# More filler products and an earlier count at the start of layer 1 of a four-layer graph kernel

## The chip, the core and the metric

The kernel runs on one core of a Trainium2 chip. TensorE (PE in the profile) does matrix products, VectorE (DVE) and ScalarE (ACT) do arithmetic on 128 partitions, GpSimd (POOL) does the same more slowly, SyncE (SP) issues DMA transfers. Each engine takes its own instructions in order and waits on semaphores that other engines raise. The metric is the device time of one execution in microseconds, and less is better. The median of three runs before the change is 498.71 us, and they lie between 497.31 and 499.81.

## The reference, cut to what matters

There are four layers. Each adds a graph operation to `x` (3327 rows of 64) and normalises the rows; all use the same dense matrix `adj` (3327 x 3327).

```python
x = _layernorm(x + _L0_gnn_ref(L0_gnn_t, x, adj))        # only row statistics of x survive
x = _layernorm(x + _L1_gnn_ref(x, adj, att_W, att_b))    # hyperbolic attention
x = _layernorm(x + _L2_gnn_ref(x, adj, W))               # two rounds of adj @ x, tanh
x = _layernorm(x + _L3_gnn_ref(x, adj, weight, bias))    # weighted by rank of neighbours
...
def _L1_gnn_ref(x, adj, att_W, att_b):
    x_tan = _logmap0(x, C)
    left = x_tan @ att_W[:D] + att_b
    right = x_tan @ att_W[D:]
    adj_att = jax.nn.sigmoid(left + right.T) * adj
    x_local = _logmap(x[:, None, :], x[None, :, :], C)
    support_t = jnp.einsum('ij,ijd->id', adj_att, x_local)
    return _proj(_expmap(x, support_t, C), C)
```

Layer 1 needs, for every row, two products with the attention weights (`left` and `right`) and functions of the row's variance. Then it makes a weight for each pair of rows: a sigmoid times `adj` times a function of the angle between the two rows.

## The kernel before, in words

The 3327 rows are padded to 26 blocks of 128. Blocks `b` and `b + 13` stand side by side as two halves, so that 13 pairs of blocks fill 128 partitions when they are turned (transposed).

The first 15 us are a preparation, written in a fixed order for all engines (`manual_schedule`): the order in the program is the order on each engine. The steps that matter here, by line:

- L1218 to L1219: three products of the identity with `center_4`, 512 columns each, into a bank `idle` that nobody reads. They run while the rows `x0` are still being loaded.
- L1225 to L1228: VectorE sums the rows and makes `xc`, the centred rows, a half at a time.
- L1244: TensorE turns the pairs of blocks of `x0` into four banks `pt`, as groups of 4, 4, 4 and 1. ScalarE copies them into `xT` (L1253). Between the first copy and the other three ScalarE squares `xc` (L1252).
- L1256 to L1264: VectorE sums the squares to the variance `v`, makes three linear functions of it (`vq`), then `low` (rows with a small variance) and `lows`, their number on each partition.
- L1267 to L1278: for each of the 13 pairs TensorE multiplies a 128 x 128 piece of `xT` with `attw_c`, which has 4 columns. These are the narrow products, into `pr`. Ahead of the fourth group stands `n_low`, a product that adds `lows` over the partitions. After the first group and after the fourth stands one more product into `idle`, of 512 and 256 columns.
- L1280 to L1290: ScalarE takes a square root, VectorE makes `t` and `r2` from it, copies `n_low` to the integer `flag` (L1285), and makes `lf` and `rb`, which read `pr`.
- L1292 to L1299: VectorE makes some more columns of 26 numbers, ending in `gas` and `aa`.

L2110 loads `flag` into a register of every engine, and L2111 branches on it: with no small norm `near_sphere` runs. There VectorE scales `lj` by `gas` (L1553), TensorE turns `lf` (L1459, `prep_left` and `first_left`), `lj` (L1481), `ri` (L1505) and makes `first_wrong` (L1491) with ordinary products, and ScalarE copies each result out of PSUM (L1515), with a sigmoid (L1373) between the copies. After that comes the loop over 104 tiles: products (L1400), angle on ScalarE (L1409), gather on VectorE (L1420 to L1424), sigmoid on ScalarE and its product with `adj` on GpSimd (L1378), and accumulation on TensorE (L1444). Layers 2 and 3 follow.

Each float product is two instructions on TensorE, each with a weight load of its own (PEld); a transpose is one.

Of the kernel before, what the change touches and what calls it, by code (L numbers as in the profile page):

```python
# [10 lines left out]
F32 = mybir.dt.float32  # L11
# [4 lines left out]
ALU = mybir.AluOpType  # L16
AX = mybir.AxisListType
PSUM = bass.MemoryType.PSUM

P = 128  # L20
# [39 lines left out]
NEAR_VAR = 0.05  # L60
# [22 lines left out]
def kernel(  # L83
# [11 lines left out]
    nc = tc.nc  # L95

    const = ctx.enter_context(tc.tile_pool(name="const", bufs=1))
    small = ctx.enter_context(tc.tile_pool(name="small", bufs=2))
# [11 lines left out]
    ident = const.tile([P, P], F32, name="ident")  # L110
# [57 lines left out]
    real = const.tile([P, NB], F32, name="real")  # L168
# [29 lines left out]
    center_4 = center.unsqueeze(1).to_broadcast([P, 4, P])  # L198
# [30 lines left out]
    def stat(tag):  # L229
        return small.tile([P, NB], F32, tag=tag, name=tag)  # L230
# [43 lines left out]
    def by_half(v):  # L274

        return v.rearrange("p (n h) d -> p n h d", h=2)
# [913 lines left out]
    with tc.tile_pool(name="l1", bufs=1) as l1:  # L1190
# [14 lines left out]
        flag = l1.tile([1, 1], I32, name="flag")  # L1205
        xc = xpool.tile([P, NB, D], F32, tag="x", name="xc")
        vec, sca = nc.vector.tensor_tensor, nc.vector.tensor_scalar
        stt = nc.vector.scalar_tensor_tensor
        with tc.tile_pool(name="l1a", bufs=1) as l1a, tc.tile_pool(
            name="l1ap", bufs=1, space=PSUM  # L1210
        ) as l1ap:
            v = l1a.tile([P, NB], F32, name="v")
            sums = l1a.tile([P, NB], F32, name="sums")
            sq = l1a.tile([P, NB, D], F32, name="sq_c")
            xT = l1a.tile([P, HALF], F32, name="xT_0")

            idle = l1ap.tile([P, 4 * P], F32, name="idle")
            for _ in range(3):  # L1218
                nc.tensor.matmul(idle, ident, center_4, start=True, stop=True)  # L1219

            pw = l1ap.tile([P, 4], F32, name="pw")
            attw_c = l1a.tile([P, 4], F32, name="attw_c")
            halves = (slice(0, None, 2), slice(1, None, 2))
            for h in halves:
                nc.vector.tensor_reduce(sums[:, h], x0[:, h, :], axis=AX.X, op=ALU.add)  # L1225
            for h in halves:
                stt(
                    xc[:, h, :], sums[:, h].unsqueeze(2).to_broadcast([P, NBH, D]), -1.0 / D,  # L1228
                    x0[:, h, :], op0=ALU.mult, op1=ALU.add,
                )  # L1230
            for h, c in zip(halves, (x0, xc)):

                nc.gpsimd.tensor_tensor(
                    lj[:, h, : D - 1], c[:, h, : D - 1],
                    c[:, h, D - 1 : D].to_broadcast([P, NBH, D - 1]), ALU.subtract,
                )

            pr = l1ap.tile([P, NBH, 2, 2], F32, name="pr")
            turned = []
            for i, g in enumerate(range(0, NBH, 4)):  # L1240
                n = min(4, NBH - g)
                pt = l1ap.tile([P, 4 * P], F32, tag="pt", bufs=4, name=f"pt_x_{g}")
                for k in range(n):
                    nc.tensor.transpose(  # L1244
                        pt[:, k * P : (k + 1) * P],
                        by_half(x0)[:, g + k].rearrange("p h d -> p (h d)"), ident,
                    )
                if i == 1:
                    nc.tensor.matmul(pw, center, attw_dg, start=True, stop=True)
                    nc.scalar.copy(attw_c, pw)  # L1250
                    for h in halves:
                        nc.scalar.activation(sq[:, h, :], xc[:, h, :], AF.Square)  # L1252
                nc.scalar.copy(xT[:, g * P : (g + n) * P], pt[:, : n * P])  # L1253
                turned.append((g, n))
            for h in halves:
                nc.vector.tensor_reduce(v[:, h], sq[:, h, :], axis=AX.X, op=ALU.add)  # L1256
            sca(vq[:, 1], v, 0.81 / D, LN_EPS, ALU.mult, ALU.add)
            sca(vq[:, 0], v, MIN_VAR, None, ALU.max)
            sca(vq[:, 2], v, 0.81 / D - 0.81, LN_EPS, ALU.mult, ALU.add)

            low = stat("low")
            stt(low, v, NEAR_VAR, real, op0=ALU.is_lt, op1=ALU.mult)
            lows = small.tile([P, 1], F32, tag="lows", name="lows")
            nc.vector.tensor_reduce(lows, low, axis=AX.X, op=ALU.add)  # L1264
            root = l1a.tile([P, 2, NB], F32, name="root")
            n_low = l1ap.tile([1, 1], F32, name="n_low")
            for i, (g, n) in enumerate(turned):  # L1267
                if i == 3:
                    nc.tensor.matmul(n_low, lows, ones, start=True, stop=True)
                for k in range(g, g + n):  # L1270
                    nc.tensor.matmul(
                        pr[:, k].rearrange("p h t -> p (h t)"), xT[:, k * P : (k + 1) * P],
                        attw_c, start=True, stop=True,
                    )
                if i in (0, 3):
                    w = 2 if i else 4
                    nc.tensor.matmul(
                        idle[:, : w * P], ident, center_4[:, :w], start=True, stop=True  # L1278
                    )
            nc.scalar.activation(root, vq[:, :2], AF.Sqrt)  # L1280
            nc.scalar.activation(warm, ones, AF.Sigmoid)
            nc.vector.reciprocal(root, root)
            t = l1a.tile([P, 2, NB], F32, name="t")
            vec(t, vq[:, :2], root, ALU.mult)
            nc.vector.tensor_copy(flag, n_low)  # L1285
            vec(t, t, root, ALU.mult)
            stt(r2, t, -3.0, root, op0=ALU.add, op1=ALU.mult)
            prs = pr.rearrange("p n h t -> p (n h) t")
            stt(lf, prs[:, :, 0], -0.5 * LOG_NORM, r2[:, 0], op0=ALU.mult, op1=ALU.mult)
            stt(rb, prs[:, :, 1], -0.5 * LOG_NORM, r2[:, 0], op0=ALU.mult, op1=ALU.mult)  # L1290

            nc.vector.reciprocal(rq, vq[:, 1:])  # L1292
            sca(rb, rb, attb_sb, None, ALU.add)
            sca(s, r2[:, 1], -0.45, None, ALU.mult)
            vec(g1, vq[:, 2], rq[:, 0], ALU.mult)
            vec(ga, vq[:, 1], rq[:, 1], ALU.mult)
            vec(gas, ga, s, ALU.mult)
            sca(lj[:, :, D - 1], ga, 2.0, -1.0, ALU.mult, ALU.add)
            sca(aa, g1, -1.0, 1.0, ALU.mult, ALU.add)  # L1299
# [867 lines left out]
```

## Time and profile before

| what | value |
|---|---|
| median of three runs | 498.71 us |
| the profiled execution, its own time | 499.74 us |
| its span, first to last instruction | 498.0 us |
| TensorE busy | 480.5 us (96%) |
| VectorE, ScalarE, GpSimd busy | 349.2, 266.3, 196.8 us |
| mean granted TensorE clock | 0.981 |

Times within the span are given in us from its first instruction. The profiled execution took 1.74 us more than its span. A busy TensorE is one that has an instruction under way; a product of 4 columns and one of 512 both count as busy. The column PEclk is the share of the full TensorE clock that was granted. In the chain of waits each line is a stretch of work that released the next one; in groups and timelines "x8" is the number of instructions, and "<-" names what ended a wait.

### The profile page before, as it was taken

How to read it: one execution, taken by the hardware profiler on the slowest of the kernel's cores; microseconds unless marked ns; L12 is line 12 of the kernel's file. 1: busy time of each engine (PE TensorE's matmuls, PEld its weight loads, DVE VectorE, ACT ScalarE, POOL GpSimd, SP SyncE). 2: the span in 40 equal slices, each digit the busy share in tenths (PEclk: the TensorE clock that was granted, in tenths of full speed). 3: DMA queues.
4: the chain of work that ended last, by engine and by line, in shares of the span. 5: the costliest groups of instructions: out<-in, count | busy, mean ns of one | idle time of the engine just before them, and what ended most of it. 6: DMA issues, size and time to landing. Idle time of an engine off the chain costs nothing.

```text
span 498.0 us, 7739 instructions
## 1 busy us (share of the span) xinstructions
PE 480.5 (96%) x2865; PEld 220.6 (44%) x2865; DVE 349.2 (70%) x600; ACT 266.3 (53%) x376; POOL 196.8 (40%) x175
## 2 busy tenths in 40 slices
PE   8999999999999999999999999999999999999991
PEld 4733333333333338643434353333345555555551
DVE  6698888878888887995363322656238999689743
ACT  4799999999999985400000000000016876666641
POOL 4299899989999991000000000000352274000000
PEclk9799999999999998999999999999999999999996
DMA  8988988887888278899999009988987699949001
GB/s 273 379 247 281 328 274 273 272 273 259 280 274 276 77 277 314 372 397 428 424 426 384 0 17 403 427 349 334 421 333 235 222 334 387 365 150 356 17 1 42
DMA packets 34186, 139.20 MB, mean 280 GB/s; under 512 B 11231, under 2 KB 13025, under 8 KB 29019
## 3 DMA queue, kind: packets, MB, share of 16 engines
q1 hardware_dynamic: 30603, 137.41, 73.9%
q0 software_dynamic: 1248, 0.64, 0.6%
q10 hardware_dynamic: 2288, 0.57, 0.6%
q8 instruction: 24, 0.39, 0.3%
q14 instruction: 23, 0.19, 0.1%
HBM read 136.93 MB, written 1.04 MB: 277 GB/s over the span
## 4 chain that ended last, share of the span: by engine, by line
PE 80%; DVE 8%; DMA 5%; issue 1%; ACT 1%; SPq 0%; POOL 0%; DVEq 0%
PE cnt L517 26%; PE pq L1400 17%; PE acc L1444 16%; PE cnt L651 5%; PE acc L883 5%; DMA at_l<-in_adjT 3%; PE acc L900 2%; DMA ah<-in_adjT 2%; PE t L452 2%; DVE mask L368 2%; DVE w L667 1%; PE both L752 1%; PE cnt L508 1%; PE pn_l L403 1%; PE pe L1735 1%
## 5 line engine op out<-in xcount | busy, mean ns | idle before, releaser
L1378 POOL TENSOR_TENSOR sg<-sg,at 128x832 f32<-128x832 f32 x88 | 131.2, 1519 | 7.6 <-ACT sg L1373 3.1
L517 PE MATMUL cnt<-at_l,lj 128*64 128x416 f32 x496 | 90.7, 515 | 0.8 <-DMA at_l<-in_adjT 0.8
L1373 ACT ACTIVATE sg<-lb,rb 128x1664 f32<-128x1664 f32 (+1 forms) x53 | 88.0, 1661 | 0.0
L1400 PE MATMUL pq<-riT,ljT 64*128 64x416 f32 x416 | 87.2, 536 | 0.2
L1444 PE MATMUL acc<-v,lj 128*64 128x416 f32 x416 | 85.1, 525 | 0.0
L1409 ACT ACTIVATE pq<-pq 128x832 f32<-128x832 f32 x104 | 83.8, 850 | 1.7 <-issue 1.6
L630 ACT ACTIVATE x<-cnt 128x416 f32<-128x416 f32 x8 | 4.1, 517 | 144.9 <-PE cnt L517 144.9
L669 ACT ACTIVATE w<-cnt 128x416 int16<-128x416 f32 x135 | 63.9, 520 | 28.3 <-PE cnt L651 26.8
L1424 DVE SCALAR_TENSOR_TENSOR v<-pq,sg 128x832 f32<-128x832 f32 x52 | 53.3, 1025 | 18.7 <-ACT pq L1409 18.3
L464 POOL DMA_DIRECT2D t_rows<-tb x4 | 4.1, 1045 | 151.0 <-DVE tb L462 151.0
L1400 PEld LDWEIGHTS pq<-riT,ljT 64*128 64x128 f32 x416 | 35.6, 186 | 49.5 <-ACT pq L1409 30.6
L517 PEld LDWEIGHTS cnt<-at_l,lj 128*64 128x64 f32 x496 | 34.3, 137 | 50.9 <-issue 48.6
L883 PE MATMUL acc<-w,s 128*128 128x416 bf16 x208 | 53.1, 339 | 0.0
L667 DVE TENSOR_SCALAR w<-cnt 128x416 int16<-128x416 f32 x73 | 42.1, 587 | 10.7 <-PE cnt L651 8.3
L1444 PEld LDWEIGHTS acc<-v,lj 128*64 128x64 f32 x416 | 26.0, 136 | 52.2 <-issue 48.4
L517 PE MATMUL cnt<-kept,lj 128*64 128x416 f32 x224 | 41.6, 514 | 0.0
L651 PE MATMUL cnt<-mask,tri 128*128 128x416 bf16 x136 | 35.6, 339 | 2.1 <-DVE w L667 2.1
L368 DVE TENSOR_SCALAR mask<-ah 128x1664 bf16<-128x1664 f32 x34 | 36.4, 1096 | 1.0 <-DMA ah<-in_adjT 1.0
L1421 DVE SCALAR_TENSOR_TENSOR pq<-pq,sg 128x416 f32<-128x416 f32 x52 | 31.2, 600 | 1.8
L445 DVE TENSOR_SCALAR tm<-at_l 128x1664 bf16<-128x1664 f32 x16 | 15.7, 1023 | 22.8 <-PE t L452 20.9
L1420 DVE SCALAR_TENSOR_TENSOR v<-pq,sg 128x416 f32<-128x416 f32 x52 | 30.2, 580 | 0.0
L1044 POOL DMA_DIRECT2D out<-hid x2 | 1.0, 514 | 73.3 <-DVE hid L1049 73.3
(321 smaller groups left out, 525.6 us busy)
## 6 DMA issues: line engine op xcount, KB each, us to landing
at_l<-in_adjT SPq DMA_DIRECT2D x27, 1664.0 KB, 12.3
at<-in_adjT SPq DMA_DIRECT2D x44, 832.0 KB, 5.8
ah<-in_adjT SPq DMA_DIRECT2D x34, 832.0 KB, 6.6
kept<-in_adjT SPq DMA_DIRECT2D x7, 1664.0 KB, 9.6
bt_l<-in_adjT SPq DMA_DIRECT2D x6, 1664.0 KB
lb<-lf_rows SPq DMA_DIRECT2D x2, 384.0 KB
mask<-t_rows SPq DMA_DIRECT2D x34, 3.2 KB
ljT<-ljT SPq DMA_DIRECT2D x4, 128.0 KB
```

What stands on the lines that cost most here:

```text
L368: nc.vector.tensor_scalar(mask[q], ahead.pop(q), 0.0, None, ALU.not_equal)
L517: nc.tensor.matmul(acc[c][h * D : (h + 1) * D, :], hw[:, slot(jb), :], blocks[jb][:, o : o + CW], start=c not in begun, stop=last, skip_gr ...
L651: nc.tensor.matmul(cnt[c][e], tri, mask[q][:, of], start=True, stop=True, skip_group_check=True,)
L667: nc.vector.tensor_scalar(to, of, 0.0, None, ALU.max)
L669: nc.scalar.activation(to, of, AF.Relu)
L883: nc.tensor.matmul(acc[h, c][:, e, :], s12[:, slot(jb)].rearrange("p t d -> p (t d)"), ws[q, c, e], start=first, stop=last,)
L1373: nc.scalar.activation(sg[:, :, of], lbs[:, :, of], AF.Sigmoid, bias=rb[:, sl : sl + 1])
L1378: nc.gpsimd.tensor_tensor(sg[:, h, of], sg[:, h, of], at[:, h, of], ALU.mult)
L1400: nc.tensor.matmul(pq[:, h, :], ljT[h != jb // NBH][rows, of], riT[rows, ch * CW : (ch + 1) * CW], start=True, stop=True,)
L1409: nc.scalar.activation(pqs[t], pqs[t], AF.Arctan, bias=ANGLE_FIRST, scale=ANGLE_STEP)
L1424: stt(w, pq, ANGLE_REST, sg, op0=ALU.add, op1=ALU.mult)
L1444: nc.tensor.matmul(accs[cp, ci][h * D : (h + 1) * D, :], lj[:, slot(jb), :], w[:, h, :], start=(jb == orders[cp][0]), stop=(jb == orders[c ...
```

## The change

The warm-up products at L1218 become 512, 512 and 256 columns instead of three times 512. `low` and `lows` are computed ahead of `vq[:, 1]`, `vq[:, 0]` and `vq[:, 2]` or between them. `n_low` stands ahead of the third group of narrow products instead of the fourth. In the second and third group a filler of 256 columns follows every second narrow product, four in all; the filler after the first group (512) and after the fourth (256) stay. VectorE copies `flag` before it makes `t` instead of after.

```diff
-            for _ in range(3):
-                nc.tensor.matmul(idle, ident, center_4, start=True, stop=True)
+            def filled(w=4):
+                nc.tensor.matmul(idle[:, : w * P], ident, center_4[:, :w], start=True, stop=True)
+
+            for w in (4, 4, 2):
+                filled(w)
...
+            low = stat("low")
+            lows = small.tile([P, 1], F32, tag="lows", name="lows")
+            stt(low, v, NEAR_VAR, real, op0=ALU.is_lt, op1=ALU.mult)
             sca(vq[:, 1], v, 0.81 / D, LN_EPS, ALU.mult, ALU.add)
             sca(vq[:, 0], v, MIN_VAR, None, ALU.max)
+            nc.vector.tensor_reduce(lows, low, axis=AX.X, op=ALU.add)
             sca(vq[:, 2], v, 0.81 / D - 0.81, LN_EPS, ALU.mult, ALU.add)
-
-            low = stat("low")
-            stt(low, v, NEAR_VAR, real, op0=ALU.is_lt, op1=ALU.mult)
-            lows = small.tile([P, 1], F32, tag="lows", name="lows")
-            nc.vector.tensor_reduce(lows, low, axis=AX.X, op=ALU.add)
             root = l1a.tile([P, 2, NB], F32, name="root")
             n_low = l1ap.tile([1, 1], F32, name="n_low")
             for i, (g, n) in enumerate(turned):
-                if i == 3:
+                if i == 2:
                     nc.tensor.matmul(n_low, lows, ones, start=True, stop=True)
                 for k in range(g, g + n):
                     nc.tensor.matmul(
                         pr[:, k].rearrange("p h t -> p (h t)"), xT[:, k * P : (k + 1) * P],
                         attw_c, start=True, stop=True,
                     )
-                if i in (0, 3):
-                    w = 2 if i else 4
-                    nc.tensor.matmul(
-                        idle[:, : w * P], ident, center_4[:, :w], start=True, stop=True
-                    )
+                    if i and k % 2:
+                        filled(2)
+                if i == 0:
+                    filled()
+                if i == 3:
+                    filled(2)
             nc.scalar.activation(root, vq[:, :2], AF.Sqrt)
             nc.scalar.activation(warm, ones, AF.Sigmoid)
             nc.vector.reciprocal(root, root)
+            nc.vector.tensor_copy(flag, n_low)
             t = l1a.tile([P, 2, NB], F32, name="t")
             vec(t, vq[:, :2], root, ALU.mult)
-            nc.vector.tensor_copy(flag, n_low)
             vec(t, t, root, ALU.mult)
```

## The prediction

> **What bounds the kernel now.** I first read the granted clock in short stretches of the opening, since the change adds products that nobody reads. Columns: busy us (and instructions) of PE, PEld, DVE, ACT, POOL, then PEclk, DMA share, GB/s.
>
> ```profile
> 4.55:7.96 3.41, 3.41 (x7) 1.35 (x6) 2.05 (x3) 0.00 (x0) 1.55 (x1) 1.00 1.11 259
> 7.96:11.37 3.41, 3.41 (x26) 2.62 (x24) 3.24 (x4) 3.02 (x6) 1.55 (x1) 1.00 1.00 418
> 11.37:14.78 3.41, 3.19 (x26) 2.77 (x26) 3.06 (x18) 2.14 (x5) 0.00 (x0) 1.00 0.98 401
> 14.78:18.20 3.42, 2.75 (x14) 2.35 (x13) 2.91 (x10) 2.16 (x3) 0.00 (x0) 0.50 1.07 334
> 18.20:21.61 3.41, 3.41 (x25) 2.75 (x23) 1.55 (x3) 1.93 (x4) 1.68 (x2) 0.50 0.97 406
> ...
> 192.28:195.69 3.41, 3.41 (x34) 3.41 (x33) 2.38 (x9) 1.86 (x5) 0.00 (x0) 1.00 0.76 218
> 195.69:199.10 3.41, 3.41 (x19) 3.41 (x18) 3.01 (x26) 2.06 (x8) 0.00 (x0) 0.50 0.97 408
> ```
>
> The clock is halved from 14.78 to 21.61 (6.83 us) and from 195.69 to 199.10 (3.41 us): both edges lie on one grid of 3.41 us, which I use for the stretches. The stretch ahead of each drop is nearly all "busy", but with narrow products. Then the chain of waits over the opening:
>
> ```profile
> 15.76 0.70 DVE lj L1553
> 16.46 0.04 issue
> 16.50 1.11 PE first_right L1481 x4
> 17.61 1.28 PE first_left L1459 x6
> 18.89 0.85 PE first_turn L1505 x4
> 19.75 1.91 PE first_wrong L1491 x16
> 21.65 0.59 PE first_turn L1505 x4
> ...
> 22.57 0.44 PE prep_fours L1481 x4
> ```
>
> TensorE at half clock is on the path: four transposes cost 0.85 to 1.11 us, and 0.44 at full clock. ScalarE then takes the copy of `first_wrong` at 21.70 and its sigmoids at 22.18, and from there the loop runs without a gap. Last, the narrow products and who reads them, in the timeline:
>
> ```profile
> 10.12 1.10 PE L1277 MATMUL idle<-both_m,ident 128*128 128x512 f32 x2
> 11.18 1.95 PE L1271 MATMUL pr<-attw_c,xT 128*128 128x4 f32 x16
> 13.06 0.19 PE L1269 MATMUL n_low<-ones,lows 128*1 128x1 f32 x2
> 13.18 0.39 PE L1271 MATMUL pr<-attw_c,xT 128*128 128x4 f32 x2
> ...
> 13.59 0.21 DVE L1287 SCALAR_TENSOR_TENSOR r<-t,root 128x52 f32<-128x52 f32 x1
> 13.91 0.19 DVE L1289 SCALAR_TENSOR_TENSOR lf<-pr,r 128x26 f32<-128x26 f32 x1
> ```
>
> The last narrow product ends at 13.57 and `lf` starts at 13.91: TensorE is only 0.34 us early. The end moves with this place: the loop's TensorE rows follow each other from 26.16 on, and at layer 1's end the chain goes from VectorE's last scaling into the transfer `at_l` (211.79, 13.94 us). So a shift at 22.18 reaches the end one for one.
>
> **The change, part by part.** *Shorter warm-up.* The first six filler instructions start about 0.85 us apart (5.49 us in all), so half of a product less ends them 0.85 sooner. The transposes of x can then start when x is there, at 6.85 (the weight load that waited for the DMA) instead of 7.47. That is worth nothing: ScalarE's squares wait for `xc`, ready at 8.75 and 9.73, and the other copies of `xT` follow them (10.56); so the second narrow group still starts at 11.18. Without that cover it would be a gain of 0.6.
>
> *The four fillers.* Full-clock price of 416 columns: the chain shows 32 such instructions of L517 in 5.74 us, two at a time, 0.36 a pair; 256 columns are 0.22, a filler of two 0.44. Its first weight load (16 loads of L1271 took 1.86, so 0.116 each) is exposed, and the one after it hidden, so no more is added. The upper bound is 0.68, the whole row of the old 256-column filler at L1277, its drain included; I take the stream, since here other work follows. Four: **1.77 us** of TensorE ahead of the last narrow product. VectorE's 0.34 of slack covers a part; `lf` needs 15.3 instead of 13.91: **+1.4 us**. Behind it on VectorE stand `rb`, the columns to `aa`, the branch and `lj` L1553; behind those TensorE's turns and ScalarE's copies and sigmoids. All move by 1.4.
>
> *Order of the count.* Short VectorE operations start 0.09 apart, so one put ahead of `vq` delays the root by 0.08; `lows` is ready 0.1 to 0.2 sooner. But `n_low` now stands behind the second group and two fillers: 11.18 + 8 x 0.116 + 0.88 = 12.99, and before it ran at 13.06. So `flag` comes at about 13.3 as before, and with it the register loads and the two `kept` transfers (SP issues them at 14.19): 0. VectorE waits there with `t` behind it, which was at 12.97: about 0.3 later, r2 at 14.0 to 14.1. The wait for `pr` until 15.3 hides all of it; without the fillers it would cost 0.2 to 0.3.
>
> *The clock.* What the fillers can buy: with full clock from 17.9 on (16.50 + 1.4), `first_right` 0.44, `first_left` 0.66, one turn 0.44 and `first_wrong` 0.96 end at 20.4; ScalarE's five copies and the wait for the first results (18.9, then copies 0.42 to 0.58 apart) end at 21.4. The sigmoid at 22.18 comes 0.8 sooner: saving 2.2, less the 1.4. If the clock falls just as now: +1.4. If it falls already among the fillers, each costs 0.88 and a narrow product twice its load: some 2 more, about +3.5.
>
> **Does the clock hold?** For each stretch I add the columns streamed (a 128-column transpose 0.11 at full clock, a product of 4 columns nothing). Share of 3.41 us with columns moving: 4.55 to 7.96 1.00 at half speed, and the clock rose; 7.96 to 11.37 0.60 (nine transposes and the 512 filler), it held; 11.37 to 14.78 0.27 (256 filler and four transposes), it fell; 14.78 to 18.20 0.70 at half speed, it stayed down; 18.20 to 21.61 0.90 at half speed, it rose; 192.28 to 195.69 0.17, it fell. So it drops somewhere between 0.27 and 0.60, and rises (half speed counted half) between 0.37 and 0.45. With one threshold for both it is about 0.4. After the change, on the same grid, 11.37 to 14.78 holds three fillers and part of the fourth, 1.57 us or 0.46, and the next 0.52 (the last filler, eight transposes, the first of `lj`). Just above: there the clock would hold.
>
> But the Trainium skill (TensorE: Matmul & The Clock Gate, Part 1) says that this window is free-running and does not start with the kernel. No row here shows a second grid; the three times before differ by 2.5 us, as they would. If the grid stands still, the sum is 499.74 - 0.8 = 498.9. If it moves, other windows count. The earlier transposes bring the 512 filler forward, to about 9.4 to 10.3 where the clock is already up. A window whose end lies from 11.9 to 12.6 then holds that filler and less than one small one, 0.25 to 0.38; one that ends from 13.3 to 14.5 holds two or three small ones and at most the rest of the large one, 0.26 to 0.39. Together that is 1.9 of 3.41 us: with the threshold at 0.4 the clock falls in nearly six of ten positions. And the execution shown was a bad one for the kernel before, 1.03 above the median: with edges at 13.1, 16.5 and 19.9 the clock is back for half of `first_wrong`, and 22.18 becomes 21.4. So against the median the clock that holds saves 0 to 0.2, and one that falls costs +1.4 to +3.5. I take the moving grid: four in ten at -0.1, six in ten spread over 1.4 to 3.5, and after the median over runs **+1.7: 500.4 us**.
>
> A second rule of that page (Part 4) speaks against the change more strongly: transposes do not count as work for the clock. Then the stretch after the fillers would be left with one filler (0.13 to 0.2) and the clock would fall at 18.2: +1.4. Here the row disagrees: without transposes 18.20 to 21.61 would be 0.50 and the clock rose, while the warm-up from 1.13 to 4.54 was 0.64 and it did not. I count them.
>
> **The rivals.**
> - *The clock holds in nearly every execution* (threshold near 0.3): 498.71 - 0.2 = 498.5, down to 497.5 if the position of the profiled run is common. For it: 0.46 and 0.52 against 0.27. Against it: the low windows at other positions. This one ends on the other side, and it decides once the lowest window's share lies above the threshold.
> - *The clock falls among the fillers, or never rises in the warm-up*: fillers at half clock give about +3.5, so 502.2. The warm-up's window loses 0.25 to 0.6 us of streaming, at half speed 0.42 to 0.46 instead of 0.50; if the rise needs more than that, everything to about 25 us runs at half clock, some +7, 505.7. For it: 0.45 is the least that raised the clock. Against it: 0.45 did.
> - *The fillers are free*, if `lf` were not waiting for TensorE: 498.71 - 2.2 = 496.5. Against it: 0.34 us of slack.
>
> **How the numbers follow.** A measurement of this kernel can tell about 0.5% (2.5 us) from no change. Forecast as told (some executions with the clock down, +0.5 to +3.2): 0.56, of which 0.14 over 2.5. Clock holds: 0.23, within 0.5%. Clock down among the fillers or in the warm-up: 0.18, nearly all over 2.5. Free fillers: 0.03, faster by about 0.5%. So faster 0.03, same 0.65, slower 0.32. The forecast's own range is 499.2 to 501.9; for 8 in 10 it reaches down into the held clock, 498.0, and up into the second rival, 503.0.
>
> **What would show it.** Four 256-column fillers in L1271's stretch, the last narrow product at about 15.1, `lf` at 15.3, and L1553 at about 17.2: the fillers' price. `n_low` near 13.1 and `flag` near 13.3: the reordering brings nothing. PEclk 1.00 from 8 to 25 with the sigmoid at 21.4 means that the clock holds; 0.50 anywhere from 12 to 22 means that it does not, and edges off 14.78 that the grid moves. I am wrong if `lf` stays before 14.3, if weight loads or fillers overlap more than I think, or if the loop absorbs the shift.

## The result, and the profile after

Over 22 executions of each kernel, taken side by side, the median went from 499.02 us to 500.09 us; the ratio is 1.0036 with a 95% interval of 1.0018 to 1.0053. (The ratios of this document are not quotients of medians: here that would be 1.0021, and the quotient of the means, 500.62 to 498.85, is 1.0035.) The change makes the kernel slower by a little, and the interval does not contain 1. The medians hide a change of shape: before, the executions lie evenly between 497.25 and 499.84. After, ten of 22 lie between 498.79 and 499.36, three between 500.09 and 500.63, and nine between 501.38 and 504.19. Those nine have a mean granted clock of 0.977 to 0.982 each, the other thirteen 0.987 to 0.993.

The profiled execution of the changed kernel took 499.36 us (span 497.6) and is one of the thirteen. The line numbers are 3 higher from here on. First the stretches of its clock grid, with the same columns as before (busy us of PE, PEld, DVE, ACT, POOL, then PEclk, DMA share, GB/s):

```profile
6.41:9.82 3.41, 3.14 (x25) 2.74 (x25) 3.41 (x4) 1.62 (x3) 1.20 (x1) 1.00 0.93 371
9.82:13.24 3.42, 2.67 (x15) 1.58 (x14) 2.96 (x9) 2.95 (x6) 1.55 (x1) 1.00 1.03 436
13.24:16.65 3.41, 3.31 (x24) 2.79 (x24) 1.78 (x12) 0.81 (x2) 0.00 (x0) 1.00 0.99 298
16.65:20.06 3.41, 2.49 (x23) 2.08 (x23) 2.94 (x9) 2.99 (x6) 0.00 (x0) 1.00 0.94 394
20.06:23.48 3.42, 3.38 (x33) 2.27 (x30) 3.09 (x6) 3.42 (x5) 1.93 (x2) 1.00 1.02 433
```

The clock stays full where it was halved before. The edges are not where they were: the clock rose at 6.41 in this execution, at 7.96 in the one before. (Ahead of that first rise PEclk reads 1.00 too, since the profile records the clock from its first change on; that TensorE runs at half clock there is seen from the warm-up, whose instructions of 512 columns start 0.85 us apart, against 0.47 in the run e4 below at full clock.) Then the path, from the timelines of TensorE, VectorE and ScalarE:

```profile
11.28 0.61 PE L1273 MATMUL pr<-attw_c,xT 128*128 128x4 f32 x4 [0.76 <-ACT xT L1256]
11.74 0.68 PE L1219 MATMUL idle<-both_m,ident 128*128 128x256 f32 x2
...
13.23 0.19 PE L1271 MATMUL n_low<-ones,lows 128*1 128x1 f32 x2
...
15.21 0.28 PE L1273 MATMUL pr<-attw_c,xT 128*128 128x4 f32 x2
```

```profile
13.46 0.15 DVE L1286 CAST flag<-n_low 1x1 int32<-1x1 f32 x1 [0.40 <-PE n_low L1271]
13.54 0.19 DVE L1288 TENSOR_TENSOR t<-vq,root 128x52 f32<-128x52 f32 x1
...
15.53 0.18 DVE L1292 SCALAR_TENSOR_TENSOR lf<-pr,r 128x26 f32<-128x26 f32 x1 [1.31 <-PE pr L1273]
...
17.38 0.68 DVE L1556 TENSOR_TENSOR lj<-lj,gas 128x504 f32<-128x504 f32 x1 [0.47 <-DVE aa L1302]
```

```profile
20.93 0.58 ACT L1518 COPY ljT<-first_wrong 128x512 f32<-128x512 f32 x1
21.42 2.57 ACT L1376 ACTIVATE sg<-lb,rb 128x832 f32<-128x832 f32 x2
```

`lf` now waits 1.31 us for TensorE, and starts at 15.53 instead of 13.91. What the fillers cost is in that bracket. The full clock then gives time back: from `lf` to the start of ScalarE's second sigmoid, the 21.42 above, it takes 5.89 us instead of 8.27, and this sigmoid starts 0.76 sooner than before (22.18). Not all of that reaches the end. The last product into `acc`, at the end of layer 1's loop, ends 0.32 sooner (190.63 against 190.95), and the span is 0.4 shorter. The missing 0.45 appears at VectorE's first `v` of the loop, here before and after the change:

```profile
25.60 1.02 DVE L1424 SCALAR_TENSOR_TENSOR v<-pq,sg 128x832 f32<-128x832 f32 x1 [0.20 <-ACT pq L1409]
25.29 1.02 DVE L1427 SCALAR_TENSOR_TENSOR v<-pq,sg 128x832 f32<-128x832 f32 x1 [0.65 <-ACT pq L1412]
```

It starts 3.42 us after the second sigmoid before, and 3.87 after. The experiments show which part of the change does this. That this execution gained and the median lost is the subject of what follows.

### The profile page after: what moved, and what is told of

It reads as the page before. It is cut to its first block, busy times and chain, and to the rows that moved or that the text cites. A ratio compares the mean times of both kernels' runs of the same rounds, so it can differ in the third digit from the quotient of the medians.

```text
span 497.6 us, 7756 instructions
## 1 busy us (share of the span) xinstructions
PE 477.7 (96%) x2873; PEld 217.6 (44%) x2873; DVE 349.4 (70%) x600; ACT 266.2 (53%) x376; POOL 196.4 (39%) x175
## 4 chain that ended last, share of the span: by engine, by line
PE 81%; DVE 9%; DMA 4%; issue 1%; ACT 1%; SPq 0%; POOL 0%; DVEq 0%; ACTq 0%
PE cnt L517 26%; PE acc L1447 16%; PE pq L1403 16%; PE cnt L651 5%; PE acc L883 5%; PE acc L900 3%; DMA at_l<-in_adjT 3%; PE t L452 2%; DVE mask L368 2%; DVE w L667 1%; PE both L752 1%; PE cnt L508 1%; DMA mask<-t_rows 1%; PE pn_l L403 1%; PE pe L1738 1%
```

## The experiments

My theory had two parts: four fillers put 1.4 us on VectorE's chain in every execution, and the clock falls or holds by where a grid of 3.41 us happens to lie. The rivals: the order of the count costs the time (`t` waits behind `flag`); the shorter warm-up sometimes fails to raise the clock; the time is lost in the later layers. Below, "before" is the kernel before, run beside each.

| run | executions | median us | lowest to highest | ratio to before (95%) |
|---|---|---|---|---|
| e1 full warm-up | 6 | 503.13 | 499.32 to 505.56 | 1.0100 (1.0071 to 1.0129) |
| e2 no fillers | 22 | 499.90 | 498.36 to 502.98 | 1.0016 (1.0003 to 1.0030) |
| e3 fillers only | 22 | 499.71 | 498.91 to 504.06 | 1.0031 (1.0012 to 1.0050) |
| e4 wide fillers | 7 | 501.53 | 501.16 to 503.82 | 1.0058 (1.0035 to 1.0081) |
| before, beside e1 to e4 | 44 | 499.56 | 497.27 to 501.69 | |
| e5 fillers off the path, one left | 22 | 499.35 | 497.74 to 504.17 | 1.0010 (0.9995 to 1.0024) |
| e6 fillers off the path | 14 | 498.75 | 497.47 to 499.34 | 0.9988 (0.9974 to 1.0002) |
| e7 short warm-up only | 14 | 499.24 | 497.69 to 500.04 | 1.0004 (0.9991 to 1.0017) |
| e8 as e1 | 12 | 500.76 | 499.15 to 503.79 | 1.0047 (1.0025 to 1.0070) |
| before, beside e5 to e8 | 49 | 499.25 | 497.48 to 500.82 | |
| e9 fillers in gaps, on the kernel before | 21 | 498.38 | 497.19 to 500.43 | 0.9982 (0.9973 to 0.9992) |
| before, beside e9 to e12 | 25 | 499.04 | 497.92 to 500.42 | |

### Three more profiles of the changed kernel: where an execution over 501 us loses its time

The kernel is the changed one, without an edit.

> The changed kernel itself, one look for the place of the clock's grid. Theory: if the execution takes under 500.5, PEclk is 1.00 from 8 to 25 us and the second sigmoid starts at 21.3 to 21.9; if it takes more than 501, PEclk is 0.50 in at least one stretch between 11 and 22 us, the fillers in it take twice their time, and the second sigmoid starts at 23 to 26. In both cases the span less that start is 475.5 to 476.5. Rival (the slow executions lose their time elsewhere, in the later layers): the start stays under 22 and the span less the start grows to 478 or more.

> The changed kernel itself, a second look for another place of the grid; the same expectation as for the first look.

> The changed kernel itself, a third look for another place of the grid; the same expectation as for the first look.

They took 500.19, 501.46 and 502.04 us. In the first the clock rose at 6.44 and stayed; the second sigmoid started at 21.53. In the other two it was halved from 13.73 to 20.55 and from 14.07 to 20.90, and the sigmoid started at 24.27 and 24.18. The stretches of the second one:

```profile
10.31:13.73 3.42, 2.66 (x17) 1.82 (x16) 2.77 (x9) 2.98 (x6) 1.35 (x1) 1.00 1.00 424
13.73:17.14 3.41, 3.41 (x14) 3.05 (x14) 0.64 (x4) 0.53 (x2) 0.00 (x0) 0.50 0.94 244
17.14:20.55 3.41, 3.31 (x14) 2.61 (x13) 2.56 (x13) 0.59 (x1) 0.00 (x0) 0.50 0.98 418
```

and its chain of waits (start, us, what):

```profile
12.98 0.54 PE idle L1219 x2
13.52 0.12 PE n_low L1271 x2
13.63 0.83 PE pr L1273 x4
14.46 1.06 PE idle L1219 x2
15.52 0.65 PE pr L1273 x4
16.17 1.06 PE idle L1219 x2
17.23 0.22 PE pr L1273 x2
17.45 1.06 PE idle L1219 x2
18.51 0.10 issue
18.61 1.94 PE prep_left L1462 x8
```

A filler takes 1.06 us in this chain instead of 0.54, and two narrow products 0.65 instead of 0.34. `lf` starts at 17.48. The fillers that were to hold the clock are now themselves the path, at twice their price. Even the last one, after the narrow products, stands ahead of `prep_left`. The span less the start of the sigmoid is 476.9, 475.4 and 476.0 in these three, and 476.2 in the first profile: within some 1.5 us the rest takes the same time, while the sigmoid comes 2.7 later when the clock falls. So the rival of the later layers falls for the executions over 501. The execution of 500.19 lay 0.4 over my bracket. Its clock held and its sigmoid came only 0.11 later than in the profile of 499.36; it was 0.26 behind at the last `cnt<-at_l` product (366.54) and 0.67 behind at the last `cnt<-mask` product (477.94). So what sets 500.1 off from 499.2 is, in this one profile, mostly in the later layers, and its cause was not found.

### Parts alone: the count and the warm-up

Without the fillers (e2):

```diff
-                    if i and k % 2:
-                        filled(2)
```

> The changed kernel without the four fillers of 256: shorter warm-up and the earlier count alone. Theory: lf at 14.1 to 14.3 (VectorE waits for n_low with t behind it, 0.2 to 0.3), the clock falls in the opening in practically every execution as before: median 499.0 to 499.5. Rival (the count ahead of the third group is the loss): 500 or more, with lf at 15 or later. Rival 2 (the fillers are the loss and the reordering a gain): 498.5 or less.

The fillers on the kernel before, with its own count and warm-up (e3):

```diff
+                    if i in (1, 2) and k % 2:
+                        filled(2)
```

> The kernel before with the four fillers alone: full warm-up, count and flag in their old places. Theory: n_low is now behind all four fillers (about 14.9), so flag comes at about 15.1, t waits behind it and lf starts at 15.6 to 15.9, against 15.5 in the changed kernel; the two kept transfers go out 1.7 us later; median 499.6 to 500.4. Rival (the reordering costs, the fillers help): faster than 498.8.

The short warm-up on the kernel before (e7):

```diff
-            for _ in range(3):
-                nc.tensor.matmul(idle, ident, center_4, start=True, stop=True)
+            for w in (4, 4, 2):
+                nc.tensor.matmul(idle[:, : w * P], ident, center_4[:, :w], start=True, stop=True)
```

> The kernel before with the warm-up shortened to 512, 512 and 256 and nothing else. Theory: no gain on VectorE's or ScalarE's chain (lf moves only with the arrival of x), and the 512 filler after the first group moves up by up to 0.6 us, so that the clock falls a little sooner in some executions: within 0.5 us of the kernel before. Rival (the short warm-up sometimes does not raise the clock): a tail over 503. Rival 2 (it lets the chain start earlier): 0.4 us or more faster.

e2: `lf` at 14.42. VectorE's centring of x started 0.26 later than in the profile before, and the other 0.25 are a wait for TensorE, whose last narrow product already fell on a halved clock (13.40 to 20.23). VectorE did not wait for `n_low`, and `r` started at 13.75, only 0.16 later than before with x 0.26 later; so the 0.2 to 0.3 that I expected the early count to cost ahead of `lf` did not come. The executions show no separate groups. The median was 0.3 over that of the kernel before beside it, above my bracket by 0.4, and the interval lies just above 1.

A part of that small loss has a place, and it is the 0.45 of the two `v` lines above. From the second sigmoid to the end of the last product into `acc`, layer 1's loop takes 168.76 us in the profiles of the kernel before, of e7 and of e9, and 169.08 in e3, which loses the difference later in the loop: the four with the old order of the count. In all ten profiles with the early count, with fillers or without and with either warm-up, it takes 169.20 to 169.23. In these ten the first `v` starts 3.86 to 3.89 us after the sigmoid, in the four others 3.42. So the order of the count costs some 0.45 us in every profiled execution, far behind the place where it was changed. Why is open: the profile names ScalarE's `pq` as what ended the wait, but that ends 3.31 to 3.35 us after the sigmoid in all of them.

e3: `lf` at 15.87, with x within 0.03 of the changed kernel's, because `flag` now comes at 15.25 behind all fillers. The median of 499.71 lies in my bracket, and the executions fall into the same two groups (15 up to 500.62, seven from 501.13 on). In its profile the clock held, though this stretch is near the limit that is worked out below:

```profile
10.06:13.47 3.41, 2.68 (x18) 2.06 (x16) 3.01 (x9) 3.13 (x6) 1.42 (x1) 1.00 1.01 429
```

So the fillers alone make the pattern. Moving the count spares `lf` some 0.3 and loses 0.45 in the loop. e7: no difference (interval 0.9991 to 1.0017), and no tail over 503; the warm-up alone is neither a loss nor a gain.

The changed kernel with the full warm-up (e1, and again as e8):

```diff
-            for w in (4, 4, 2):
+            for w in (4, 4, 4):
```

> The changed kernel with the warm-up back at three products of 512. Theory (fillers cost 1.4 us on VectorE's chain, the clock falls in those executions whose window finds too little streaming): lf and L1553 stand where they stood in the changed kernel, within 0.2 us; but the 512 filler after the first group comes some 0.6 us later, which closes part of the hole before 11.2, so fewer executions fall: median 499.2 to 499.8, and the executions over 503 go. Rival 1 (the shorter warm-up is harmless and the fillers are all): 500.1, spread as the changed kernel. Rival 2 (the shorter warm-up sometimes fails to raise the clock, and this is the whole loss): 498.0 to 498.8, no execution over 501.

> The same kernel as e1 once more, since six executions gave 503.1 against my 499.2 to 499.8 while e3, with the same fillers and warm-up, gave 499.7 in 22. Theory (where the clock's grid happens to lie decides, and e1 drew badly): most executions at 499 to 500, some at 501 to 504, as in e3. Rival (the full warm-up with the early count is really worse): a median above 502 again.

Both medians missed. I expected the longer warm-up to help and it did not: taken together, eight of the 18 executions took up to 501.13 and ten from 502.06 to 505.56. In the changed kernel nine of 22 lie over 501.3, in e3 seven of 22 over 501. With numbers like these a real difference and a bad draw can't be told apart; that stays open. What it excludes is that the short warm-up causes the loss. Both profiled executions of this kernel were ones in which the clock held, with `lf` at 15.89 and 15.85; that is 0.36 and 0.32 later than in the changed kernel, and x was 0.35 and 0.32 later.

### The price of a filler

```diff
-                        filled(2)
+                        filled()
```

on e1's kernel: fillers of 512 columns between the narrow products.

> The changed kernel with four fillers of 512 instead of 256 columns and the full warm-up. Theory: another 4 x 0.44 = 1.77 us ahead of the last narrow product, all of it on VectorE's chain: lf at 17.2 to 17.4, and the clock holds in every execution, so a narrow spread (under 1.5 us) and a median of 500.7 to 501.3. Rival (the fillers lie in slack and only the clock counts): 499 with the same narrow spread.

The median of 501.53 lay 0.2 above my bracket. The narrow group came: five of seven executions between 501.16 and 501.69, with 501.35 in their middle, 2.2 above the changed kernel's lower group, while the kernel before beside them was 0.5 longer than in the changed kernel's comparison. That leaves 1.6 to 1.7 of the 1.77 that I worked out, so the price is paid at the end nearly in full. But the clock does not always hold: in the profiled execution it fell at 12.28 for 3.41 us, and `lf` came at 19.18.

```profile
8.87:12.28 3.41, 2.65 (x17) 1.82 (x16) 3.28 (x6) 2.92 (x5) 1.55 (x1) 1.00 0.97 414
12.28:15.70 3.42, 3.42 (x8) 1.53 (x7) 0.90 (x6) 1.73 (x3) 0.00 (x0) 0.50 0.90 321
```

The stretch ahead of the fall has the 512 filler and the pause before the second group; in this execution more filler behind that pause could not mend it.

### Fillers where TensorE waits anyway

If the price is only paid ahead of the last narrow product, fillers elsewhere should be free. Both kernels start from the changed one, with its count and its warm-up; the filler at `i == 1` is in e5 alone.

```diff
                 if i == 0:
                     filled()
+                    filled()
-                    if i and k % 2:
-                        filled(2)
+                if i == 1:
+                    filled(2)
                 if i == 3:
-                    filled(2)
+                    filled(3)
...
-                def alone(make, b, n):
+                def alone(make, b, n, fill=0):
                     pt = n1p.tile([P, 4 * P], F32, name=f"first_{make.__name__}_{b}")
+                    if fill:
+                        nc.tensor.matmul(pt[:, : fill * P], ident, center_4[:, :fill], start=True, stop=True)
...
-                    rows_j = alone(right, 9, 4)
+                    rows_j = alone(right, 9, 4, 4)
```

> The changed kernel with its fillers moved to where TensorE waits anyway: a second filler of 512 columns after the first group (it has 0.9 us to wait for ScalarE's copy), one of 256 after the second group instead of four, 384 instead of 256 columns after the last group, and one of 512 in the bank of first_right, ahead of its transposes, while VectorE makes lj. Theory (a window with less than about 0.35 of streaming drops the clock, and every filler ahead of the last narrow product costs its length on VectorE's chain): lf at 14.0 to 14.3, every window from 8 to 25 us at 0.38 or more, clock held in all or nearly all executions: median 497.4 to 498.3, none above 500.5. Rival (the loss comes from the order of the count and the shorter warm-up, which are kept here): 499.5 to 500.

> The same without the one filler between the second and third group. Theory: lf some 0.1 to 0.3 sooner than with it, but windows that span the narrow products hold 0.26 to 0.32 and fall in part of the executions: median 497.5 to 499.5 with a tail to 501. Rival (the threshold is lower than 0.3, or any filler near helps): as fast as e5 or faster, with no tail.

e5's median missed by over 1 us and came close under the rival's 499.5. (e6, with the same order and warm-up, is 0.6 faster, so these two do not explain e5's median.) In the profiled execution (498.49) all went as expected: `lf` at 14.64 with x 0.48 later than before, the clock full from 7.41 on, and the second sigmoid at 20.54. Eight executions, this one among them, took 497.74 to 498.49; of the other 14, 13 lie between 498.89 and 500.52, most of them with a mean clock of 0.984 to 0.985. I had left a hole: on this layout a window from 11.64 to 15.05 has one filler of 256 and part of the 384 one, 0.27 by my count. That this is where those 14 fell was not seen in a profile. e6 has a smaller spread and a lower median than e5 and no tail, which is what its rival said, though not for the rival's reason of a lower threshold: in its profile the clock fell at 15.44 and was back at 18.85:

```profile
12.03:15.44 3.41, 3.23 (x25) 2.52 (x25) 2.92 (x21) 1.84 (x4) 0.00 (x0) 1.00 1.07 354
15.44:18.85 3.41, 3.41 (x12) 2.27 (x11) 2.94 (x8) 2.16 (x3) 0.00 (x0) 0.50 0.94 335
```

With TensorE streaming through the second stretch, half clock lasted 3.41 us and not 6.83. But its 512 filler ahead of `first_right` then ran at half clock too, until 17.9, and `lj` was ready at 16.7. So the last kernel has 256 there, and nothing else of the change (e9):

```diff
-                if i in (0, 3):
-                    w = 2 if i else 4
+                for w in {0: (4, 4), 3: (3,)}.get(i, ()):
...
-                    rows_j = alone(right, 9, 4)
+                    rows_j = alone(right, 9, 4, 2)
```

> The kernel before, its count and warm-up untouched, with fillers only where TensorE waits: a second one of 512 after the first group, 384 instead of 256 columns after the last group, 256 in the bank of first_right ahead of its transposes. Theory: nothing is put ahead of the last narrow product, so lf stays at 13.9 to 14.0 (later only by the arrival of x); the clock still falls in part of the executions, for one stretch of 3.41 us instead of two: median 0.3 to 1.0 us under the kernel before, none above 500.5. Rival (only an unbroken clock helps): equal to the kernel before.

498.38 us against 499.04, 0.9982 of the kernel before (0.9973 to 0.9992), and the only kernel here whose interval lies below 1: it beats both. It also keeps the old order of the count and so doesn't lose the 0.45 in the loop. In one step my text was wrong. `lf` came at 14.74, some 0.65 late, because with the full warm-up the second 512 filler ran until 12.1, past the copy it was to wait for (11.3). The clock fell at 15.18 and rose at 18.60. Whether the short warm-up or a smaller filler in that place would save this 0.65 wasn't tried.

## Why the prediction was right

*The fillers' price: right, and a little low.* I had 1.77 us of TensorE and +1.4 for `lf`. From the start of the second narrow group to the end of the last product it took 4.21 us (11.28 to 15.49) against 2.39, so 1.82; `lf` moved by 1.62, to 15.53 instead of the forecast 15.3, and 0.10 of that is x that came later.

*Slack and count: right as far as `lf`, mis-sized behind it.* `n_low` at 13.23 and `flag` at 13.46 brought nothing sooner; VectorE waited 0.40 for it with `t` behind, and the later wait of 1.31 for `pr` hid all of that. But I had put the order of the count at 0, and it costs the 0.45 us in the loop.

*The held clock: right.* The sigmoid was to start at 21.4 and started at 21.42. Two small errors cancel there: `lf` came 0.2 later than forecast, and the way from it to the sigmoid was 0.2 shorter than my 6.1. In all seven profiles in which the clock was full from `lf` on, this way took 5.88 to 5.91 us.

*The moving grid: right.* In the 14 profiles of this case the clock first rose anywhere between 5.20 and 8.36. The rule of the Trainium skill (TensorE: Matmul & The Clock Gate, Part 1) that the window is free-running is what the runs show. The profiled execution before, with two stretches at half clock and 499.74 us, was 0.7 above the median of the 22; in e7 and e9, which keep its order, the drop in the profile lasted one stretch.

*The threshold: mis-sized.* I put it at about 0.40, and so let the clock fall in six of ten executions. By the same count of columns streamed, good to about 0.02, it held in the opening at 0.36 (e3, e5), 0.38 (e1, e8) and about 0.40 (the changed kernel), and fell at 0.34 (e4 and e6), 0.33 and 0.27 (the two executions over 501) and 0.31 (e9). It is about 0.35, and by the mean clock of each execution it held in some 13 of 22. The limit is not sharper than the count: over all stretches at full clock in the 14 profiles none below 0.36 held, but two that fell later in the kernel had 0.37 and 0.38 (before 487.69 in the changed kernel, before 196.09 in e9).

*What a fallen clock costs: mis-sized the other way.* +1.4 to +3.5 was forecast; the nine executions lie 2.4 to 5.2 above the median before. The profiles at 501.46 and 502.04 show how: when the clock falls at 13.7 or 14.1 the two fillers that are left and the last one run at half speed, and `lf` comes some 1.8 later than in the profile at 500.19, where the clock held. The group at 503.3 to 504.2 has a mean clock of 0.977 to 0.979 instead of 0.981 or 0.982; I estimate from this some 3 to 4 us more at half clock, about one stretch. It was not caught in a profile.

*The median: near by luck.* The 500.4 was to be an execution that had lost its clock, since six of ten were to lose it. But nine of 22 lost it, and the measured median, 500.09, is two executions with mean clocks of 0.993 and 0.992, in which it held. By my own working those gain 0 to 0.2. The 0.45 of the order of the count is in them, as in all the others; what else sets them off, going by the profile at 500.19, lies mostly in the later layers and is unexplained. The mean is the better test of the mechanism: by my mix (0.4 at -0.1, 0.6 at 2.45, the middle of its range) it should lie an estimated 1.4 us over the median before, and it lies 1.6 over it (500.62 against 499.02). Falls were rarer than forecast, and each cost more.

*The rivals.* The clock that holds in nearly every execution did not come true, though where it holds the median is 499.2, close to nothing gained. The fall among the fillers is real, in up to four of ten executions, which the median of 22 does not show. The free fillers are refuted by the 1.31 us that `lf` waits.

*Transposes.* I had counted them as work for the clock, against the Trainium skill (TensorE: Matmul & The Clock Gate, Part 4), which says that they do not count in the same way. In the changed kernel's stretch from 13.24 to 16.65 the transposes of `prep_left` are a minor part. The stretch from 16.65 to 20.06 decides; it consists of transposes but for the first products of `first_wrong` from 19.80 on:

```profile
16.14 1.06 PE L1462 MATMUL prep_left<-ident,lf 128*128 128x128 f32 x8
18.12 0.66 PE L1484 MATMUL first_right<-ident,lj 128*128 128x128 f32 x4 [0.92 <-DVE lj L1556]
18.61 0.82 PE L1462 MATMUL first_left<-ident,lf 128*128 128x128 f32 x6
19.27 0.60 PE L1508 MATMUL first_turn<-ident,mT 128*128 128x128 f32 x4
19.80 1.09 PE L1494 MATMUL first_wrong<-ident,lj 128*64 128x128 f32 x16
```

The clock held after it. With transposes it has about 0.6 of its time streamed, without them it would have less than 0.1, and a stretch of 0.34 was already too little elsewhere. For these float transposes the measurement goes against the page, and it decides.

## What to carry to other kernels

In this kernel a filler that holds the clock was free only where the engine waited. One that stands ahead of a product whose reader is waiting costs its full length, and twice that in the executions where it fails to hold the clock. Before judging such a change compare several executions: with a grid that lies elsewhere each time, one profile shows one draw, and the mean clock of each execution tells which kind it was. And compare profiles stretch by stretch down to the end: the 0.45 us of the early count stand over 10 us behind the lines that were moved.

## What the runs showed of the hardware

Narrow products keep TensorE "busy" and do not keep its clock: of 128 x 4 they follow each other 0.112 us apart, each with a weight load, and after stretches with 3.19 and 3.41 us busy (11.37 to 14.78 and 192.28 to 195.69 before) the clock fell. It fell after one stretch of 3.41 us with less than about 0.35 of it streamed. In the opening it came back after one stretch where that was filled (0.98 of it streaming in e6, 0.96 in e9) and after two where it was not (0.51 in the first, from 13.73 to 17.14); in between, at 0.70 (e4, one stretch) and 0.73 (before, two), the runs don't separate the two cases. A filler of 256 columns took 0.54 us in the chain at full clock and 1.06 at half.
